# Two mixers and two FFNs on one core: the order of work at the borders, and the place of the state's scaling in the second mixer

## The chip, the core and the metric

The kernel runs on one core of a Trainium2 chip. The metric is the device time of one execution in microseconds (us), as a median over runs. A core has these engines, each with an instruction queue of its own that is worked off strictly in order: PE (matrix products and transposes, results into PSUM), DVE (vector work), ACT (activations, copies), POOL (further vector work, without PSUM) and SP (it issues DMA transfers). An instruction that waits for another engine holds up everything behind it in its own queue. Which engine ends its wait is seen in the profile behind an arrow, for instance "<-DVE u_b L474".

## What is computed

The input x is 4 batches of 1024 rows with 512 columns. Four layers follow each other, each of them added to x:

```python
x = x + mixer_a(layernorm(x))     # 16 heads, state 64, convolution over 4 rows
x = x + ffn(layernorm(x))
x = x + mixer_b(layernorm(x))     # 64 heads, state 128, convolution over 4 rows
x = x + ffn(layernorm(x))         # the same weights
```

A mixer projects the row to a gate z, to channels that go through a short convolution and a silu (h, B and C), and to one step size dt per head. Then a recurrence runs along the rows of a batch, for each head:

```python
state = state * exp(dt * A) + dt * h * B      # outer product
y     = C . state + D * h
```

y is gated with silu(z), normalized (in mixer b the norm comes first and the gate after it), and projected back to 512 columns. The FFN takes the last row of every batch, turns it in four steps of a small network into a "thought", projects that, and adds gate(x) * thought to all rows, then normalizes:

```python
thought = layer_norm(x)[:, -1, :] @ agg_w + agg_b
for _ in range(4):
    thought = thought + gelu(layer_norm(thought) @ d1_w + d1_b) @ d2_w + d2_b
out = x + sigmoid(x @ gate_w + gate_b) * (thought @ bc_w + bc_b)
result = layer_norm(out)
```

## The kernel before

**Stages.** The rows are cut into 32 tiles of 128 (8 to a batch). Mixer A runs from 0 to about 1195 us, the first FFN to about 1388, mixer B to about 2865, the second FFN to the end. Between the stages x goes through DRAM.

**A mixer** works in groups of two tiles ("chunks" c = 0, 1). For each group there is a *norm* (lines 389 to 441: statistics, a root on POOL, line 417 on DVE, the normalized rows on ACT in line 419, transposes on PE) and a *front* (443 to 628: the projections on PE, in pieces; each piece ends with a yield). The front's pieces are gates ("pz", a tanh on ACT, z on DVE in line 541) and convolutions ("pc" on PE, a first tap on ACT in line 470, three taps on DVE in line 474, then a silu). The small products of dt ("pd", line 503) are strung between the large ones. At the end of a front the running sums of dt * A go to DRAM, and *lay_sums* (641) lays them into tables called past and upto, which PE reads.

*chunk* (762) does the recurrence of 128 rows in closed form. Mixer A has wide heads (CG = 2), mixer B narrow ones (CG = 4), and for B the order is this:

1. *decays(0)* (781): PE forms the exponents of the decay masks L of a quarter of the heads in four PSUM banks ("seg"), ACT takes their exponentials (805).
2. The tail of the chunk before (658): the projection back, "pout" and "ssq" on PE.
3. *from_state* (840), in all chunks but the first of a batch: PE multiplies C with the state into two banks "po" (846), DVE scales them by the decay of each row into "yo" (850), two multiplications.
4. On POOL the state and a copy of h ("hdr") are scaled for the next state. Then the first yield: pieces of the next group's front are put in here, until the numbers that they yield have used up the chunk's.
5. *weigh(L0)* (809 to 812): DVE multiplies the masks by the products of B and C, two halves. Behind it come decays(1), the next step of the tail (684 to 690: the residual x and its statistics), a yield with front pieces, and weigh(L1).
6. *open_y* (855): PE turns yo into y's bank (859), and *inner* (817, 828) adds the products of L and h. Masks 2 and 3, the closing of y and the new state ("pst", 897, 908) follow.

So the order on PE, DVE, ACT and POOL inside a mixer is written out by hand: the code's order is the queue's, and no planner changes it. SP's order, and that of the code outside of the manual_schedule blocks, is set by a scheduler. A mixer has seven PSUM banks for all products but y; a product that finds no free bank waits for the reader of the one that it is given.

**At the kernel's start** the tables' constants are made on DVE: eleven reductions of the identity into flags (190), two corrections, two pasts (201, 204) and the flags of upto (*lay_flags*, 208). Of upto there are two, with four sets each; mixer A needs set 0, mixer B all. The call for sets 1 to 3 is in the first FFN (1096), but on the chip all of them run at the start, from 10.4 to 17.0 us, since the scheduler moves them there. Then comes the first norm and the first front, with the whole of mixer A's output weight w_out scaled by its norm weights on ACT in eight instructions ahead of it (317).

**The first FFN** turns twelve tiles (the last of the 32, *filling*) to gates while the thoughts are formed, each of them a transpose (1184), four passes of the gate weight (1196), a bias (1208), a tanh and a store ("sgd"); their last steps are done in mixer B's norm. Then the thought is projected (1225), goes out to DRAM (1229) and comes back on all partitions ("hbc", 1238). The other 20 tiles go through *Tile*, a pipeline of steps over turns: turned, projected, biased, tanh, weighed with hbc (1278), added, measured, centered (1301), left (1304, 1305).

Of the kernel before, what the change touches and what calls it, by code (L numbers as in the profile page):

```python
# [72 lines left out]
def hybrid_kernel(  # L73
# [106 lines left out]

    eye = ident.rearrange("p (r w) -> p r w", w=32)
    flags = const.tile([P, 2 * HB + 3], F32, tag="flags", name="flags")
    for i, at in enumerate(
        [slice(2 + h + 10 * lo, 7 + h + 10 * lo, 4) for lo in (0, 1) for h in range(HB)]
        + [slice(10 * lo, 10 * lo + 2) for lo in (0, 1)]
        + [slice(20, 21)]
    ):
        nc.vector.tensor_reduce(flags[:, i : i + 1], eye[:, :, at], mybir.AxisListType.XY, ALU.add)  # L190
    heads4, first2, row20 = flags[:, :HB], flags[:, 2 * HB : 2 * HB + 1], flags[:, 2 * HB + 2 :]
    nc.vector.scalar_tensor_tensor(
        heads4, flags[:, HB : 2 * HB], 1.0 / LO_SCALE, heads4, ALU.mult, ALU.add
    )
    nc.vector.scalar_tensor_tensor(
        first2, flags[:, 2 * HB + 1 : 2 * HB + 2], 1.0 / LO_SCALE, first2, ALU.mult, ALU.add
    )
    pasts, sums = [], []
    for i in range(2):
        past = const.tile([P, SETS, P], F16, tag=f"past{i}", name=f"past_{i}")  # L200
        nc.vector.tensor_scalar_mul(
            past.rearrange("p t s -> p (t s)"), first2.to_broadcast([P, SETS * P]), -1.0
        )
        nc.vector.tensor_scalar(past[:, :, 64:], past[:, :, 64:], row20, None, ALU.add)
        upto = const.tile([P, SETS, HB, P], F16, tag=f"upto{i}", name=f"upto_{i}")
        pasts.append(past)
        sums.append(upto)
    def lay_flags(sets):
        for upto in sums:
            for t in sets:  # L210
# [6 lines left out]
                    ALU.mult,  # L217
                    ALU.add,
                )

    lay_flags(range(MIX_A.heads // 16))

    def rsqrt(v):

# [24 lines left out]
    def mixer(m, in_w, conv_w, conv_b, dt_bias, A_log, Dv, norm_w, out_w, src, dst, first, stats, last_steps={}):  # L249
# [18 lines left out]
        with stack:  # L268
# [43 lines left out]
            nc.vector.tensor_scalar_min(Ab, Ab, A_LOG_MAX)  # L312
            nc.scalar.activation(Ab, Ab, AF.Exp)
            nc.vector.tensor_scalar_mul(Ab, Ab, -A_SCALE)

            for e in range(KE):
                nc.scalar.activation(w_out[:, e, :], w_out[:, e, :], AF.Identity, scale=nw[:, e : e + 1])

# [441 lines left out]
            def chunk(f, c, following):  # L762
# [72 lines left out]
                        )  # L835
                        started[cg] = True

                tmps = []

                def from_state():  # L840

                    pos = []
                    for half in range(2):
                        rows, hsl = state_at(half)
                        po = mm(f"po_{tag}_{half}")
                        nc.tensor.matmul(po, Cc[rows, cols], state["S"][rows, hsl], start=True, stop=True)  # L846
                        pos.append(po)
                    for half, po in enumerate(pos):
                        tmp = wk.tile([P, 512], F32, tag="yo", name=f"yo_{tag}_{half}", bufs=2)
                        nc.vector.tensor_mul(  # L850
                            heads_of(tmp), heads_of(po), over_head(el[:, half * HALF : (half + 1) * HALF], P, HALF)
                        )
                        tmps.append(tmp)
# [74 lines left out]
                yield 2.0  # L928
                weigh(L0)
                if CG == 4:  # L930
                    L1 = decays(1)
                    next(last, None)
                    yield 2.2
                    weigh(L1)
                    py, on = open_y(0)
                    for half in range(2):
                        inner(0, L0, half, py, on)
                    L2 = decays(2)
                    yield 3.0
                    weigh(L2)  # L940
                    for half in range(2):
                        inner(1, L1, half, py, on)
                    close_y(0, py)
                    to_state()
                    yield 2.2
                    L3 = decays(3)
                    yield 2.8
                    weigh(L3)
                    py, on = open_y(1)
                    for half in range(2):  # L950
                        inner(2, L2, half, py, on)
                    yield 2.2
                    for half in range(2):
                        inner(3, L3, half, py, on)
                    close_y(1, py)
                else:
                    next(last, None)
                    yield 2.5
                    to_state()
                    yield 2.0  # L960
                    for half in range(2):
                        py, on = open_y(half)
                        inner(0, L0, half, py, on)
                        close_y(half, py)
                        yield 3.8
# [14 lines left out]
            with tc.manual_schedule(  # L980
                engines={
                    mybir.EngineType.PE,
                    mybir.EngineType.DVE,
                    mybir.EngineType.Activation,
                    mybir.EngineType.Pool,
                }
            ):
                fs = [Group(*groups[0]), Group(*groups[1])]
                for _ in norm(fs[0], None):
                    pass  # L990
                for _ in front(fs[0], fs[1]):
                    catch_up()
                lay_sums(fs[0], 0)
                for n in range(len(groups)):
                    if n + 2 < len(groups):
                        fs.append(Group(*groups[n + 2]))
                    f, ahead, behind = (fs + [None, None])[n : n + 3]
                    pieces = front(ahead, behind) if ahead is not None else iter(())
                    due = 0.0
                    for c in range(GC):  # L1000
                        following = (f, c + 1) if c + 1 < GC else (None if ahead is None else (ahead, 0))
                        for us in chunk(f, c, following):
                            due += us
                            while due > 0.0:
                                waiting, later_on[:] = later_on[:], []
                                piece = next(pieces, None)
                                for step in waiting:
                                    step()
                                if piece is None:
                                    break  # L1010
                                due -= piece
                            catch_up()
                    for _ in pieces:
                        catch_up()
                state.pop("fold")()
                for _ in state["tail"]:
                    catch_up()
# [3 lines left out]
    def ffn(r, src, dst, stats, filling, bias_on_pe):  # L1021
# [5 lines left out]
        CG = P // 32  # L1027
        KQ = KF // CG
        leaves = r == 0
        stack = ExitStack()  # L1030
        with stack:
            wk = stack.enter_context(tc.tile_pool(name=f"wk_f{r}", bufs=1, reuse_waits="tile"))
# [58 lines left out]
            nc.vector.tensor_copy(ones4, ident[:, 0:NB])  # L1091
            for g in range(1, CG):
                nc.vector.tensor_add(ones4, ones4, ident[:, 32 * g : 32 * g + NB])

            if leaves:
                lay_flags(range(MIX_A.heads // 16, SETS))

            def to_columns(src, n, name):

# [100 lines left out]


            kept = {}
            for i in filling:
                tag = f"{r}_{i}"
                xi = ahead[i] if i in ahead else load_tile(i, f"x_f{tag}")
                ps = project_gate(i, copy_turned(i, turn_tile(i, normed(i, xi, f"xn_f{tag}"))))
# [35 lines left out]


            class Tile:
                def __init__(self, i, resumed):
                    self.i, self.resumed = i, resumed
                    self.tag = f"{r}_{i}"
                    self.x = load_tile(i, f"x_{'g' if resumed else 'f'}{self.tag}")

# [17 lines left out]
                        nc.vector.tensor_add(self.th, self.th, gb)  # L1267

                def tanh(self):
                    if self.resumed:  # L1270
                        self.th = p_c.tile([P, D], F32, tag="c", name=f"th_{self.tag}")
                        nc.scalar.activation(self.th, kept[self.i], AF.Tanh, scale=0.5)
                    else:
                        nc.scalar.activation(self.th, self.th, AF.Tanh, scale=0.5)

                def weigh(self):
                    self.sg = wk.tile([P, D], F32, tag="sg", name=f"sc_{self.tag}", bufs=4)
# [49 lines left out]
            for n, one in enumerate(others):  # L1327
                order.append(one)
                while behind and len(behind) * len(others) > (len(others) - 1 - n) * len(filling):
                    order.append(behind.pop(0))  # L1330
            tiles = {}
            with tc.manual_schedule(
                engines={
# [6 lines left out]
                for t in range(-2, len(order) + 4):  # L1340
                    if t + 2 < len(order):
                        tiles[t + 2] = Tile(*order[t + 2])
                    for step, turn in turns:
                        if t - turn in tiles:
                            step(tiles[t - turn])

            def last_step(i, xi):
# [99 lines left out]
```

## Time and profile before

| | us |
|---|---|
| median of 3 runs | 3091.79 (3088.93 to 3094.5) |
| the profiled execution | 3096.08 |
| its span | 3094.4 |
| busy: PE / DVE / ACT / POOL | 2772.5 / 2094.4 / 1254.0 / 736.2 |
| PE busy from 1440 to 2803 us (mixer B) | 1225.8 of 1363.0 |
| PE busy from 1302 to 1379 us (20 tiles of the first FFN) | 76.5 of 77.0 |
| PE idle ahead of mixer B's first transposes, 1388.24 us | 9.75 |
| PE's first instruction of the kernel starts at | 18.05 |

A line of the timeline has the start, the duration, the engine, the line of the code, the operation, what it writes and reads with the partitions and elements, how often, and in brackets how long the engine stood idle before it and what ended that. Where several instructions of one line follow each other, they are drawn together (x3), with the time of all. A name like po_b or pc_a is the tile's with the mixer's letter. A line of waits has the waiting instruction, the one that it waited for, and the total, the number and the longest of the waits. A duration in the timeline reaches to the end of an instruction's writing, so the next one of the same engine may start a little before it.

### The profile page before, as it was taken

What the parts mean: (1) busy time and instruction counts of PE and PEld (TensorE: products, weight loads), DVE (VectorE), ACT (ScalarE), POOL (GpSimd) and SP (SyncE); (2) the same over time, 40 slices, a digit from 0 to 9 for tenths busy, and PEclk for the clock granted to TensorE, in tenths of its full rate; (3) what the DMA queues carried; (4) which work ended last, traced back from release to release, by engine and by line L of the source; (5) the groups of instructions that cost most, each with busy time, mean ns of one, the idle gap of its engine ahead of it and who ended that gap; (6) DMA issues with size and microseconds to landing.
All of it is one profiled execution on the core that took longest, in us unless ns stands there. A gap on an engine that the chain in (4) does not pass through costs nothing. (4 is left out here: it accounts for less than half of the span.)

```text
span 3094.4 us, 46185 instructions
## 1 busy us (share of the span) xinstructions
PE 2772.5 (90%) x17156; PEld 1775.0 (57%) x17156; DVE 2094.4 (68%) x4417; ACT 1254.0 (41%) x2874; POOL 736.2 (24%) x839
## 2 busy tenths in 40 slices
PE   6999999999999998989999889999888998898986
PEld 5666666666666664347665656666555665554332
DVE  4677666667766663286677777776787777876358
ACT  3333433333334333255344444444444443444245
POOL 1222122112222221170221112112223212212157
PEclk9999999999999998999999999999999999998999
DMA  3000000000000014430000000000000000001423
GB/s 115 9 20 20 16 16 16 16 16 16 23 17 16 13 67 167 162 124 10 20 13 20 19 17 11 20 20 20 20 25 16 26 20 19 17 10 72 167 87 108
DMA packets 92960, 124.27 MB, mean 40 GB/s; under 512 B 38728, under 2 KB 42328, under 8 KB 92736
## 3 DMA queue, kind: packets, MB, share of 16 engines
q1 hardware_dynamic: 80960, 98.23, 9.9%
q10 hardware_dynamic: 9792, 16.82, 1.4%
q0 software_dynamic: 1984, 6.26, 0.6%
q8 instruction: 137, 2.24, 0.3%
q14 instruction: 87, 0.71, 0.1%
HBM read 84.54 MB, written 36.72 MB: 39 GB/s over the span
## 5 line engine op out<-in xcount | busy, mean ns | idle before, releaser
L347 PE MATMUL pc_b<-xnT_b,w_in_b 128*128 128x259 f32 x1280 | 356.3, 404 | 22.3 <-DVE u_b L474 22.3
L347 PE MATMUL pc_a<-xnT_a,w_in_a 128*128 128x259 f32 x1152 | 312.0, 395 | 0.0
L812 DVE TENSOR_TENSOR L_b<-L_b,Gm_b 128x1024 f32<-128x1024 f32 x256 | 308.6, 1248 | 2.9 <-ACT L_b L805 2.9
L347 PE MATMUL pz_a<-xnT_a,w_in_a 128*128 128x256 f32 x1024 | 300.1, 407 | 0.7 <-ACT xnT_a L436 0.7
L347 PE MATMUL pz_b<-xnT_b,w_in_b 128*128 128x256 f32 x1024 | 294.0, 395 | 3.5 <-ACT xnT_b L436 3.5
L805 ACT ACTIVATE L_b<-seg_b 128x512 f32<-128x512 f32 x512 | 262.9, 599 | 65.5 <-PE seg_b L798 63.8
L347 PEld LDWEIGHTS pc_b<-xnT_b,w_in_b 128*128 128x128 f32 x1280 | 228.4, 199 | 103.0 <-issue 41.6
L474 DVE SCALAR_TENSOR_TENSOR u_b<-pc_b,cw_b,u_b 128x256 f32<-128x256 f32 x480 | 231.4, 482 | 82.3 <-ACT u_b L470 70.9
L669 PE MATMUL pout_a<-w_out_a,h_a 128*128 128x512 f32 x512 | 253.3, 642 | 34.9 <-DVE u_a L474 34.9
L1196 PE MATMUL g_ps<-gw,xnT_f 128*128 128x512 f32 x512 | 249.7, 625 | 6.5 <-DMA gw<-in_L_ffn_gate_w 4.2
L828 PE MATMUL py_b<-L_b,hdt_b 128*32 128x128 f32 x4096 | 161.4, 289 | 91.8 <-DVE L_b L812 89.5
L474 DVE SCALAR_TENSOR_TENSOR u_a<-pc_a,cw_a,u_a 128x256 f32<-128x256 f32 x432 | 208.2, 482 | 50.2 <-ACT u_a L470 39.1
L669 PE MATMUL pout_b<-w_out_b,h_b 128*128 128x512 f32 x512 | 236.1, 604 | 0.0
L347 PEld LDWEIGHTS pc_a<-xnT_a,w_in_a 128*128 128x128 f32 x1152 | 195.0, 191 | 69.1 <-issue 23.7
L881 POOL TENSOR_TENSOR h_b<-h_b,z_b 128x256 f32<-128x256 f32 x128 | 91.1, 733 | 468.4 <-ACT sq_b L880 468.4
L347 PEld LDWEIGHTS pz_a<-xnT_a,w_in_a 128*128 128x128 f32 x1024 | 168.5, 193 | 39.0 <-issue 8.6
L347 PEld LDWEIGHTS pz_b<-xnT_b,w_in_b 128*128 128x128 f32 x1024 | 167.0, 191 | 40.1 <-issue 18.2
L470 ACT ACTIVATE u_a<-pc_a,cb_a,cw_a 128x256 f32<-128x256 f32 x144 | 81.1, 564 | 263.8 <-PE pc_a L347 199.1
L828 PEld LDWEIGHTS py_b<-L_b,hdt_b 128*32 128x32 f32 x4096 | 106.2, 113 | 141.2 <-DVE L_b L812 74.0
L669 PEld LDWEIGHTS pout_a<-w_out_a,h_a 128*128 128x128 f32 x512 | 99.3, 204 | 146.3 <-issue 143.6
L1196 PEld LDWEIGHTS g_ps<-gw,xnT_f 128*128 128x128 f32 x512 | 94.5, 198 | 121.2 <-issue 115.7
L669 PEld LDWEIGHTS pout_b<-w_out_b,h_b 128*128 128x128 f32 x512 | 92.4, 190 | 99.3 <-issue 99.1
(320 smaller groups left out, 4945.8 us busy)
## 6 DMA issues: line engine op xcount, KB each, us to landing
d<-in_L_ffn_d_w SPq DMA_DIRECT2D x4, 2048.0 KB
x_f<-xa SPq DMA_DIRECT2D x32, 256.0 KB
xb<-x_b ACTq DMA_DIRECT2D x32, 256.0 KB
x_f<-xb SPq DMA_DIRECT2D x32, 256.0 KB
x_a<-in_L_attn_a_x SPq DMA_DIRECT2D x30, 256.0 KB
xa<-x_a ACTq DMA_DIRECT2D x30, 256.0 KB
out<-x_f SPq DMA_DIRECT2D x22, 256.0 KB
xf<-x_f SPq DMA_DIRECT2D x20, 256.0 KB
```

Source lines behind the costliest of these rows:

```text
L347: nc.tensor.matmul(*args, **kw)
L470: nc.scalar.activation(u, ps[:, 0:GT], AF.Identity, bias=cb[:, j : j + 1], scale=cw[:, j, 0:1])
L474: nc.vector.scalar_tensor_tensor(u, ps[:, k : k + GT], cw[:, j, k : k + 1], u, ALU.mult, ALU.add)
L669: nc.tensor.matmul(pout, f.hs[e // 2][:, e % 2, cols], w_out[:, e, :], **on)
L805: nc.scalar.activation(L[:, r], sg[r0 + r], AF.Exp)
L812: nc.vector.tensor_mul(Lr, Lr, Gm.unsqueeze(1).to_broadcast([P, 2 * HB, P]))
L828: nc.tensor.matmul(py[cg * CT : (cg + 1) * CT, e % 4, :], hdt[:, h // HC, u : u + HC, :], Ls[half][:, r, hq, :], start=not started[cg], st ...
L881: nc.gpsimd.tensor_mul(yh, yh, zs[half * 2 + r][:, :, cols])
L1196: nc.tensor.matmul(ps, xnT[:, k, :], gw[:, k, :], start=(k == 0), stop=(k == KD - 1 and not bias_on_pe))
```

## The change

Four edits:

1. At the start, the flags and pasts become a function *lay_constants*, called behind the first norm; set 0 of upto follows it, and sets 1 to 3 are laid behind the first front and its lay_sums.
2. The scaling of w_out becomes a generator *weigh_rows*: one of the eight instructions after each piece of the first front of a mixer, from the seventh piece on.
3. In mixer B the scaling of the state's part (line 850) is a function of its own, *scale_state*, and is called after weigh(L0). Mixer A calls it where it was.
4. In the first FFN the last two of the twelve gates are no longer made ahead of the thought's projection but as gate-only tiles at the end of the pipeline.

```diff
-    for i, at in enumerate(
...
-    lay_flags(range(MIX_A.heads // 16))
...
+    def lay_constants():
+        eye = ident.rearrange("p (r w) -> p r w", w=32)
...
-            for e in range(KE):
-                nc.scalar.activation(w_out[:, e, :], w_out[:, e, :], AF.Identity, scale=nw[:, e : e + 1])
+            def weigh_rows():
+
+                for e in range(KE):
+                    nc.scalar.activation(w_out[:, e, :], w_out[:, e, :], AF.Identity, scale=nw[:, e : e + 1])
+                    yield
...
-                tmps = []
+                pos, tmps = [], []
 
                 def from_state():
 
-                    pos = []
                     for half in range(2):
                         rows, hsl = state_at(half)
                         po = mm(f"po_{tag}_{half}")
                         nc.tensor.matmul(po, Cc[rows, cols], state["S"][rows, hsl], start=True, stop=True)
                         pos.append(po)
+                    if CG < 4:
+                        scale_state()
+
+                def scale_state():
                     for half, po in enumerate(pos):
                         tmp = wk.tile([P, 512], F32, tag="yo", name=f"yo_{tag}_{half}", bufs=2)
...
                 weigh(L0)
                 if CG == 4:
+                    scale_state()
                     L1 = decays(1)
...
-                for _ in front(fs[0], fs[1]):
+                if first:
+                    lay_constants()
+                    lay_flags(range(TS))
+                weighing = weigh_rows()
+                for at, _ in enumerate(front(fs[0], fs[1])):
                     catch_up()
+                    if at >= 6:
+                        next(weighing, None)
+                for _ in weighing:
+                    pass
                 lay_sums(fs[0], 0)
+                if first:
+                    lay_flags(range(TS, SETS))
...
+        last = 2 if leaves else 0
...
-            if leaves:
-                lay_flags(range(MIX_A.heads // 16, SETS))
-
...
-            for i in filling:
+            for i in filling[: len(filling) - last]:
...
                 def tanh(self):
-                    if self.resumed:
+                    if self.gate_only:
+                        self.keep()
+                    elif self.resumed:
...
+                def keep(self):
+
+                    sg = wk.tile([P, D], F32, tag="sg", name=f"sg_{self.tag}", bufs=4)
+                    nc.scalar.activation(sg, self.th, AF.Tanh, scale=0.5)
+                    kept[self.i] = dr.tile([P, D], F32, tag=f"sg{self.i}", name=f"sgd_{self.tag}")
+                    nc.sync.dma_start(kept[self.i], sg)
...
+            order += [(i, False, True) for i in filling[len(filling) - last :]]
+            gate_steps = (Tile.turn, Tile.project, Tile.add_bias, Tile.tanh, Tile.copy, Tile.normalize)
...
-                        if t - turn in tiles:
+                        if t - turn in tiles and (not tiles[t - turn].gate_only or step in gate_steps):
                             step(tiles[t - turn])
```

The two programs have the same instructions on PE, DVE, ACT, POOL and SP; only their order differs.

More of the change, by code (lines that the diff above doesn't have):

```diff
@@ L175, in hybrid_kernel @@
     SETS = max(MIX_A.heads, MIX_B.heads) // 16
-    eye = ident.rearrange("p (r w) -> p r w", w=32)
     flags = const.tile([P, 2 * HB + 3], F32, tag="flags", name="flags")
-    for i, at in enumerate(
[L186 to L190, printed above, removed]
-    heads4, first2, row20 = flags[:, :HB], flags[:, 2 * HB : 2 * HB + 1], flags[:, 2 * HB + 2 :]
@@ L192, in hybrid_kernel @@
[L192 to L202, printed above, removed]
-        )
[L204 to L207, printed above, removed]
+    heads4, first2, row20 = flags[:, :HB], flags[:, 2 * HB : 2 * HB + 1], flags[:, 2 * HB + 2 :]
@@ new lines, in hybrid_kernel @@
+    pasts = [const.tile([P, SETS, P], F16, tag=f"past{i}", name=f"past_{i}") for i in range(2)]
+    sums = [const.tile([P, SETS, HB, P], F16, tag=f"upto{i}", name=f"upto_{i}") for i in range(2)]
+    def lay_constants():
+        eye = ident.rearrange("p (r w) -> p r w", w=32)
+        for i, at in enumerate(
+            [slice(2 + h + 10 * lo, 7 + h + 10 * lo, 4) for lo in (0, 1) for h in range(HB)]
+            + [slice(10 * lo, 10 * lo + 2) for lo in (0, 1)]
+            + [slice(20, 21)]
+        ):
+            nc.vector.tensor_reduce(flags[:, i : i + 1], eye[:, :, at], mybir.AxisListType.XY, ALU.add)
+        nc.vector.scalar_tensor_tensor(
+            heads4, flags[:, HB : 2 * HB], 1.0 / LO_SCALE, heads4, ALU.mult, ALU.add
+        )
+        nc.vector.scalar_tensor_tensor(
+            first2, flags[:, 2 * HB + 1 : 2 * HB + 2], 1.0 / LO_SCALE, first2, ALU.mult, ALU.add
+        )
+        for past in pasts:
+            nc.vector.tensor_scalar_mul(
+                past.rearrange("p t s -> p (t s)"), first2.to_broadcast([P, SETS * P]), -1.0
+            )
+            nc.vector.tensor_scalar(past[:, :, 64:], past[:, :, 64:], row20, None, ALU.add)
@@ L1244, in ffn, with __init__ @@
             class Tile:
-                def __init__(self, i, resumed):
-                    self.i, self.resumed = i, resumed
+                def __init__(self, i, resumed, gate_only=False):
+                    self.i, self.resumed, self.gate_only = i, resumed, gate_only
                     self.tag = f"{r}_{i}"
```

## The prediction, made before the changed kernel ran

> **What bounds the kernel now.** I read the page first, then the waits of PE and DVE inside the second mixer, then the timelines of the places that the diff touches. The page puts PE at 90% busy, DVE at 68%, ACT at 41%: PE sets the time, so a saved or added microsecond counts only where PE stands still. That happens at the borders (the start, the seam between the first FFN and mixer B) and, in small doses, in every chunk of mixer B. These are PE's longest waits in mixer B between 1440 and 2803 us (total, times, longest):
>
> ```profile
> PE py_b L828 <- DVE L_b L812: 81.0, 87, 4.8
> ...
> PE pc_b L347 <- DVE u_b L474: 22.3, 15, 1.5
> ```
>
> So in mixer B PE's first lack is the weighed mask L of line 812, which DVE makes. Anything put ahead of a weighing on DVE is to be suspected, anything taken from ahead of it is welcome. The change does both, at different places.
>
> **Mixer B: the state's scaling (two multiplications of line 850) goes behind the first weighing.** Before, DVE does them as soon as PE has made po. The question is whether DVE had something else to do there. DVE in an odd chunk (start, duration, instruction, idle before it and what ended it):
>
> ```profile
> 1922.30 0.42 DVE L971 TENSOR_TENSOR sq_b<-sq_b 128x256 f32<-128x256 f32 x1
> 1925.31 0.69 DVE L850 TENSOR_TENSOR yo_b<-po_b,ea_b 128x512 f32<-128x512 f32 x1 [2.59 <-PE po_b L846]
> ...
> 1929.45 1.52 DVE L474 SCALAR_TENSOR_TENSOR u_b<-pc_b,cw_b,u_b 128x256 f32<-128x256 f32 x3 [2.59 <-ACT u_b L470]
> ...
> 1932.34 2.35 DVE L812 TENSOR_TENSOR L_b<-L_b,Gm_b 128x1024 f32<-128x1024 f32 x2
> 1934.61 0.14 DVE L684 TENSOR_SCALAR rs_b<-rs_b 128x1 f32<-128x1 f32 x1
> ...
> 1938.50 2.35 DVE L812 TENSOR_TENSOR L_b<-L_b,Gm_b 128x1024 f32<-128x1024 f32 x2
> ```
>
> The two scalings sit in a hole: 2.59 us of idleness ahead, 2.59 us behind (1.7 to 2.9 in the other chunks), because the next DVE work is the front's convolution, which waits for ACT and PE. The weighing stays behind that convolution in both programs. So the hole gets larger and the weighing at 1932.34 starts no sooner. In the new place, between 1934.61 and the second weighing, DVE is dense. Two scalings of 0.69 us hold DVE 0.61 each (a 0.69 us z at 1885.17 is followed by the next instruction at 1885.78): 1.22 us later for line 684, for the residual and its statistics, and for the second weighing. PE in the same chunk:
>
> ```profile
> 1931.12 0.68 PE L347 MATMUL pc_b<-xnT_b,w_in_b 128*128 128x259 f32 x2 [1.49 <-DVE u_b L474]
> ...
> 1933.39 0.60 PE L859 MATMUL py_b<-ident,yo_b 128*128 128x128 f32 x4
> ...
> 1939.77 0.64 PE L828 MATMUL py_b<-L_b,hdt_b 128*32 128x128 f32 x16 [1.10 <-DVE L_b L812]
> 1940.90 0.65 PE L828 MATMUL py_b<-L_b,hdt_b 128*32 128x128 f32 x16 [0.49 <-DVE L_b L812]
> ```
>
> Line 859 turns the scaled state into y, so it now waits for the scaling: from 1933.39 to about 1935.3 (1934.61 + 0.69). That by itself puts only PE's next 6 us back. What lasts is the next wait: PE is at 1939.77 already 1.10 us early for the second weighing, and this comes 1.22 us later. From 1942 to 1968 PE has no further wait, so nothing takes it back: **+1.22 us** an odd chunk.
>
> An even chunk (DVE, then PE):
>
> ```profile
> 1885.78 2.35 DVE L812 TENSOR_TENSOR L_b<-L_b,Gm_b 128x1024 f32<-128x1024 f32 x2
> ...
> 1895.17 1.52 DVE L474 SCALAR_TENSOR_TENSOR u_b<-pc_b,cw_b,u_b 128x256 f32<-128x256 f32 x3 [1.08 <-ACT u_b L470]
> ```
> ```profile
> 1888.04 0.61 PE L859 MATMUL py_b<-ident,yo_b 128*128 128x128 f32 x4
> ```
>
> The weighing ends at 1888.05, the first scaling at 1888.74, so line 859 starts some 0.8 us late and with it the pc products behind it on PE. DVE's own 1.22 are partly swallowed by its idle 1.08 at 1895.17, but not below the 0.8 by which that convolution's pc is late. Later PE waits there (0.94 + 0.49 for the third weighing) hang on DVE, so the 0.8 stays: **+0.8 us**.
>
> There are 28 chunks with an earlier state. Two, in the last group, have no front between po and the weighing: there L's weighing really goes into the wait for po (4.81 and 7.41 us long), and of PE's waits for L812 (1.75 and 1.42 in one, 0.51, 0.49 and 2.50 in the other) I take 2 us off each: -4. The other 26 are 15 odd and 11 even: 15 x 1.22 + 11 x 0.8 = 27.1. Together **+23**. Bounds: -4 if PE gains the 26 delays back elsewhere; +61 if each pays 2.5, its 1.22 and another 1.3 by the banks: po's two PSUM banks are held 7 to 9 us longer, and the next pc then takes a bank that is freed by line 679 (1932.27) and not by the convolution (end 1930.97). I keep near the middle, since that 1.3 lies within the wait of line 859. A gain from a DVE that no longer stands before po is excluded in the 26 by the idle behind the scaling, 1.7 us or more everywhere.
>
> **The start.** One row each of DVE, ACT, ACT and DVE:
>
> ```profile
> 17.00 0.22 DVE L417 SCALAR_TENSOR_TENSOR mv_a<-mv_a 128x1 f32<-128x1 f32 x2
> ```
> ```profile
> 17.18 1.52 ACT L419 ACTIVATE xn_a<-x_first,mv_a 128x512 f32<-128x512 f32 x2 [11.56 <-DVE mv_a L417]
> ...
> 35.84 5.01 ACT L317 ACTIVATE w_out_a<-w_out_a,nw_a 128x512 f32<-128x512 f32 x8 [15.19 <-DMA w_out_a<-in_L_attn_a_out_proj_w]
> ```
> ```profile
> 47.91 0.69 DVE L396 BATCH_NORM_STATS2 st_a<-x_a 128x6 f32<-128x512 f32 x1
> ```
>
> The norm's last small step, line 417, stands behind all the flags (9.47 to 17.0). Put ahead of them it needs only POOL's root (done at 10.4): 6.6 us earlier for xn, the transposes and the first gates. ACT then meets no scaling of w_out (wait until 35.84, then 5.01) before its first tanh: 40.75 becomes about 24.5, and DVE, idle for 10.02 us before 41.35, goes on to line 396, which needs the next two tiles of x. These were issued on SP behind w_out; the DMA moved 237 GB/s in 34-36, 91 in 36-38 and 8 in 38-40 us, so they land at about 36.5. From 47.91 on DVE is dense up to 66.8 and the rest follows it: 47.91 - 36.5 = 11.4 earlier. The eight scalings (0.63 each) now stand between ACT's convolution starts; I charge 0.9 for the ones that come ahead of a u. The twelve flag instructions of sets 1 to 3 (4.5 us) go behind the first front, where DVE is idle from 76.56 to 81.65; without that cover they cost up to 4.5. **-10.5** (-12 to -6).
>
> A sentence of the Trainium skill reads differently here: "TensorE: Matmul & The Clock Gate", Part 1, has PE at full clock after some 3.4 us of busy time, whereas two pz and two pd take 1.28 us all the way from 20.7 to 30.9 and 0.65 after 75, with a granted clock of 1.00 shown. By the page, as an estimate, these 10.2 us would end some 3.4 us sooner; since x lands at 36.5, the sum is the same by either.
>
> **The end of the first FFN.** PE, and the window in which thoughts turn into the broadcast row (its last columns are PE's clock, the DMA share and GB/s):
>
> ```profile
> 1371.23 7.25 PE L1196 MATMUL g_ps<-gw,xnT_f 128*128 128x512 f32 x16
> 1388.24 1.94 PE L434 MATMUL tpx_b<-ident,xn_b 128*128 128x128 f32 x8 [9.75 <-DVE sign_b L331]
> ```
> ```profile
> 1286.00:1302.00 16.00, 14.56 (x49) 6.27 (x49) 3.63 (x6) 4.27 (x8) 0.00 (x0) 1.00 0.89 338
> ```
>
> PE does the same work, only two gates (7.1 us at 1288.35, and their transposes) go from ahead of the broadcast to behind the last whole tile. That tile's long tail on DVE, ACT and POOL (mixer B's first PE work waits for its end, 9.75 us) then runs beside the gates; what remains behind PE's end is a bias (0.70), a tanh, a centering (0.69) and leaves of 1.4: about 3.9 us. That is -5.8. On the other side the row hb goes out and back by DMA (issue 1299.75 to the reload at 1301.5 and its landing), now some 7 us earlier, when w_in_b and w_out_b are still on their way (0.89 busy, 338 GB/s, until about 1299); the first weighing waits for it, PE for its bank, 0.8 us. **-5** (-7 to -2).
>
> Against this edit speaks a line of the Trainium skill, "Trainium Kernel Development and Optimization", Key Constraints: all queues share the same 16 DMA engines. Taken as a strict line-up, hb would come no earlier than now and, as an estimate, half the gain would go; the trace has nothing that shows it.
>
> **The scaling of w_out in mixer B**, 1394.60 to 1399.61 on ACT, was beside PE's first gates and is now spread over the front's pieces: +0.5 (0 to 1.5; without cover 5.0).
>
> **The sum.** -10.5 - 5 + 0.5 + 23 = +8. The profiled execution took 3096.1 us (span 3094.4 and 1.7 around it); it is 4.3 above the median of the three runs. On the median, 3091.8 + 8 = **3100**.
>
> **Rivals.**
> - *The delays are swallowed (faster).* In the 26 chunks the scaling's 1.22 us fall into DVE's later gaps (1.08 before a convolution; 2.01 and 1.53 before the z of odd chunks), and PE's waits behind them shrink as much. For it: DVE is idle some 11 us a chunk. Against it: the L waits come before those gaps. Scaling at 0 gives 3091.8 - 15 = 3077; full gain in the last group 3073. It decides from the point where the move costs under 9 us in all, a third of my 27.
> - *The banks bite (slower still).* po held longer stops seg or pc for another 1 us: 26 more, 3126. For it: PE already waits 22.3 us for banks read by line 474.
> - *The borders bring half*: x late, hb held up by the weights: -8 in place of -15, 3107.
>
> **Chances.** My forecast 0.50, swallowed 0.26, banks 0.17, borders 0.07. Three tenths of my own case's spread (+-10) lie within 0.2% of the time, 6 us, about what can be told from no change; so faster 0.26, same 0.15, slower 0.59. The range goes from swallowed (3072) to most of the banks (3122).
>
> **What would show it.** Right: line 419 at about 10.6, line 396 at about 36.5; 3.9 and not 9.75 us before the first tpx_b; the wait "py_b L828 <- L812" up from 81 towards 100, a new wait of py_b L859 for the scaling; the idle before u_b in odd chunks 6.7 and not 2.59 us (both holes and the scalings in one). Wrong: L812 starting sooner than 7 us behind po, or PE's waits in mixer B not growing.

## The result and the profile after

The changed kernel takes 3110.95 us (median of 4 runs, 3108.26 to 3113.98) against 3091.72: ratio 1.0062, 95% interval 1.0046 to 1.0077, so 14 to 24 us slower. The forecast was 3100, slower by 8, with a range from 3072 to 3122.

The profiled execution (span 3106.6 us) can be cut at two instructions of PE: the first transpose of the first FFN and the first one of mixer B.

| stage | before | after | difference | forecast |
|---|---|---|---|---|
| to the first FFN (the start) | 1198.91 | 1186.56 | -12.3 | -10.5 |
| first FFN (the gates) | 189.33 | 185.11 | -4.2 | -5 |
| mixer B (the scaling, w_out) | 1476.9 | 1507.2 | +30.3 | +23.5 |
| second FFN to the end | 229.3 | 227.7 | -1.6 | 0 |

The borders gained about what they should (the start's 12.3 is more than its mean over the runs, see below), and the moved scaling took it back twice over. Where in mixer B it did so looks different from what was foretold. PE's waits there, from 1420 to 2860 us:

```profile
PE py_b L828 <- DVE L_b L812: 71.8, 68, 4.8
PE seg_b L788 <- DVE u_b L474: 27.3, 15, 1.9
...
PE pc_b L347 <- DVE rs_b L679: 9.8, 15, 0.7
```

Over the same window of the kernel before, the wait for the masks was 89.5 us: it has *fallen*, while the forecast had it rise. A new one has come, of seg for a bank that the convolution frees. In all, PE stands still in mixer B for 162.9 us and not 157.2, which is 6 us of the 30. The other 24 are in PE's busy time (1319.7 to 1344.3 us) with the same instructions. An odd chunk shows how. DVE first:

```profile
1927.53 1.52 DVE L474 SCALAR_TENSOR_TENSOR u_b<-pc_b,cw_b,u_b 128x256 f32<-128x256 f32 x3 [8.42 <-ACT u_b L470]
...
1930.42 2.35 DVE L812 TENSOR_TENSOR L_b<-L_b,Gm_b 128x1024 f32<-128x1024 f32 x2
1932.69 1.28 DVE L853 TENSOR_TENSOR yo_b<-po_b,ea_b 128x512 f32<-128x512 f32 x2
...
1937.77 2.35 DVE L812 TENSOR_TENSOR L_b<-L_b,Gm_b 128x1024 f32<-128x1024 f32 x2
```

As foretold, the hole ahead of the convolution is now in one piece (8.42 us here; 6.72, as foretold, in an odd chunk in which PE makes po at full clock), the first weighing starts no sooner behind it, and the second one is later: 7.35 us behind the first, 6.16 before. PE beside it:

```profile
1929.11 0.41 PE L788 MATMUL seg_b<-later,ident 64*64 64x256 bf16 x4 [1.73 <-DVE u_b L474]
1929.44 0.40 PE L798 MATMUL seg_b<-upto,past 21*128 21x512 f16 x4
1930.56 0.83 PE L347 MATMUL pc_b<-xnT_b,w_in_b 128*128 128x259 f32 x2 [0.72 <-DVE rs_b L679]
...
1931.39 1.07 PE L347 MATMUL pc_b<-xnT_b,w_in_b 128*128 128x259 f32 x2
...
1940.18 0.64 PE L828 MATMUL py_b<-L_b,hdt_b 128*32 128x128 f32 x16 [0.19 <-DVE L_b L812]
```

Two pc products take 1.07 us here, 0.60 before. The windows of this stretch (the columns are the stretch, its length, five engines' busy time, PE's granted clock, DMA share, GB/s) say why:

```profile
1930.00:1932.00 2.00, 1.45 (x5) 1.16 (x6) 1.97 (x5) 1.93 (x4) 1.42 (x1) 0.75 0.00 0
1932.00:1934.00 2.00, 2.00 (x8) 1.41 (x7) 2.00 (x4) 0.00 (x0) 0.04 (x1) 0.50 0.00 0
1934.00:1936.00 2.00, 2.00 (x39) 1.50 (x37) 1.81 (x6) 1.27 (x3) 0.00 (x0) 0.90 0.13 51
```

PE's clock is halved from 1931.0 to 1934.4 (such a stretch is called a *spell* below), behind waits of 0.45, 1.73 and 0.72 us. So when PE gets to the second mask it hardly waits (0.19 us, where it was 1.10 + 0.49): it has been slow in the meantime. Over windows of 4 us, what each lacks of the full clock, doubled, adds up to 104 us at half clock in mixer B before and 150 after.

That leaves two readings, and the profile alone can't decide between them. **Theory DVE queue** (the forecast's): the scalings put 1.2 us more into DVE's dense stretch, so every second mask is 1.2 us later, and the slow clock only fills time in which PE would have waited. **Theory banks and clock** (the rival): po's two banks, held until the scaling, stop PE; its clock falls, and that is the loss.

### The profile page after: what moved, and what is told of

It is laid out like the page before. It is cut to its first block, busy times and chain, and to the rows that moved or that the text cites. A ratio compares the mean times of both kernels' runs of the same rounds, so it can differ in the third digit from the quotient of the medians.

```text
span 3106.6 us, 46192 instructions
## 1 busy us (share of the span) xinstructions
PE 2793.6 (90%) x17156; PEld 1791.2 (58%) x17156; DVE 2090.1 (67%) x4417; ACT 1253.4 (40%) x2874; POOL 734.5 (24%) x839
## 5 line engine op out<-in xcount | busy, mean ns | idle before, releaser
L347 PE MATMUL pc_b<-xnT_b,w_in_b 128*128 128x259 f32 x1280 | 378.8, 422 | 15.6 <-DVE rs_b L679 9.8
L347 PEld LDWEIGHTS pc_b<-xnT_b,w_in_b 128*128 128x128 f32 x1280 | 238.4, 208 | 100.9 <-issue 38.6
```

The lines of the kernel that those rows point to most:

```text
L347: nc.tensor.matmul(*args, **kw)
```

## The experiments

Mixer B's length, PE's idle time in it and the time at half clock are from the profiled run of each kernel; the last two columns are times from po to po in the second batch (odd chunks 1, 3 and 5, even chunks 2 and 4).

| kernel | median us | ratio to before, 95% interval | mixer B | PE idle | half clock | odd chunks | even chunks |
|---|---|---|---|---|---|---|---|
| before | 3091.72 | | 1476.9 | 157.2 | 104 | 41.87 41.88 41.87 | 46.78 46.67 |
| after | 3110.95 | 1.0062 (1.0046-1.0077) | 1507.2 | 162.9 | 150 | 43.07 44.77 43.50 | 47.95 47.85 |
| e1 scaling only | 3122.20 | 1.0091 (1.0076-1.0107) | 1508.1 | 163.4 | 156 | 43.07 43.67 44.77 | 47.97 47.87 |
| e2 borders only | 3078.78 | 0.9954 (0.9939-0.9969) | 1476.3 | 159.0 | 99 | 41.87 41.87 41.87 | 46.76 46.68 |
| e3 occupancy | 3147.54 | 1.0175 (1.0158-1.0192) | 1528.9 | 200.5 | 122 | 43.20 44.14 44.15 | 48.10 48.00 |
| e4 banks | 3114.97 | 1.0066 (1.0051-1.0082) | 1498.1 | 164.3 | 129 | 42.15 42.95 43.97 | 47.22 46.94 |
| e5 wait | 3099.03 | 1.0022 (1.0010-1.0034) | 1482.0 | 165.7 | 98 | 41.99 42.01 42.00 | 46.90 46.81 |
| e6 last group | 3077.72 | 0.9949 (0.9933-0.9965) | 1473.6 | 160.1 | 92 | 41.88 41.88 41.88 | 46.77 46.67 |
| e7 fill | 3108.68 | 1.0054 (1.0035-1.0072) | 1506.9 | 164.0 | 81 | 43.08 43.07 43.08 | 47.98 47.88 |
| e8 one moved | 3110.52 | 1.0063 (1.0042-1.0084) | 1497.7 | 159.0 | 136 | 42.47 44.17 42.49 | 47.37 47.28 |
| e9 weighing behind | 3073.38 | 0.9932 (0.9916-0.9948) | 1474.2 | 147.1 | 140 | 42.39 42.12 43.67 | 45.43 45.33 |
| e10 weighing ahead | 3036.88 | 0.9815 (0.9799-0.9830) | 1435.7 | 133.0 | 85 | 41.29 40.36 40.36 | 45.43 45.34 |

The ratios are to the runs of the kernel before on the same chip (its median was 3091.72, 3095.33, 3091.34 and 3097.14 us in the four groups of runs).

**e1: the scaling alone**, the kernel before with the third edit only.

> The kernel before with the move of the state's scaling alone. In the changed kernel mixer B got 30 us longer (from the first tpx_b to the second FFN's first transpose). All theories that see this loss in the moved scaling expect about 3092 + 30 = 3122 us. If part of the loss came from the other three edits (another phase of the clock, w_out's scaling in pieces), it is less: 3105 to 3115.

Mixer B is as long as in the changed kernel (1508.1 and 1507.2). The whole loss is the scaling's.

**e2: the borders alone**, the changed kernel with the scaling back.

```diff
-                    if CG < 4:
-                        scale_state()
+                    scale_state()
...
-                    scale_state()
                     L1 = decays(1)
```

> The changed kernel with the scaling of the state back at its old place, so the three border edits alone. In the trace the first FFN starts 12.4 us earlier and mixer B another 4.2, so theory one (the borders gain, the scaling loses) expects 3092 - 16.6 + 0 to 3 for w_out's pieces in mixer B: about 3076. If the borders' gain is lost again in mixer B whatever the scaling does: 3085 to 3092.

3078.78, 16.5 us under the median of the kernel before on its chip (14 by the ratio), near the 16.6 that was expected. Mixer B has its old length.

**e3: DVE's queue alone.** Everything stays at its place, but two statistics over the scaled state are put behind the first weighing.

```diff
                 if CG == 4:
+                    for half, tmp in enumerate(tmps):
+                        spare = wk.tile([P, 8], F32, tag="spare", name=f"spare_{tag}_{half}", bufs=1)
+                        nc.vector.bn_stats(spare[:, 0:6], tmp)
                     L1 = decays(1)
```

> The kernel before, with two idle-purpose statistics over the scaled state (128x512, about 0.6 us each on DVE) behind the first weighing in mixer B; their results are used by nothing. PSUM banks, PE's waits for yo and the scaling's place are as before: only DVE's queue is longer there. Theory DVE queue (1.2 us later for the second weighing, and PE waits for that in every chunk): 28 x 1.2 = 34, so about 3125. Theory banks (the loss comes from po's two PSUM banks being held, which stops PE and lets its clock fall): little, 3092 to 3100.

The two take 1.42 us together and hold DVE 1.33; the even chunks of the table and its first odd chunk, in which PE's clock stays up, are longer by exactly that, and the wait for the masks is what grows:

```profile
PE py_b L828 <- DVE L_b L812: 116.4, 98, 5.2
```

It cost more than expected, 52 us and not 34. The difference is in chunks with spells (the two odd ones of the table pay 2.27, single ones elsewhere up to 3.9). In such a chunk PE waits in one piece for the second mask and is slow just behind it:

```profile
1952.56 2.21 PE L828 MATMUL py_b<-L_b,hdt_b 128*32 128x128 f32 x32 [2.43 <-DVE L_b L812]
```

These 32 products take 1.08 us at full clock; from 1952.5 to 1955 the granted clock was 0.50.

**e4: the held banks alone.**

```diff
                 if CG == 4:
+                    for half, po in enumerate(pos):
+                        spare = wk.tile([P, 8], F32, tag="spare", name=f"spare_{tag}_{half}", bufs=1)
+                        nc.vector.tensor_copy(spare[:, 0:1], po[:, 0:1])
                     L1 = decays(1)
```

> The kernel before with the scaling at its old place, but behind the first weighing DVE also copies one column of each po (results unused, about 0.1 us each), so that only the two PSUM banks stay held as long as in the changed kernel. Theory DVE queue: 26 x 0.2 at most, 3092 to 3097. Theory banks: in the 15 odd chunks PE waits about 1.7 us for a bank that line 474 frees, and its clock halves now and then: 3092 + 15 x 1.2 to 15 x 2, about 3110 to 3122.

The kernel is some 20 us slower, with the same new waits as in the changed kernel:

```profile
PE seg_b L788 <- DVE u_b L474: 27.3, 15, 1.9
PE pc_b L347 <- DVE rs_b L679: 10.3, 15, 0.7
```

In the table the even chunks lose 0.3 to 0.4, the odd ones anything between 0.3 and 2.1, as the clock falls or not. Not all of that is the banks' doing: the two copies hold DVE for 0.26 us, about what the chunks without spells lose, or 7 us over 28 chunks. So the banks by themselves cost some 14 us. Each of the two mechanisms is enough for a loss, and e3 and e4 don't add up to e1 (52 + 21 against 31).

**e5: the wait of line 859 alone.**

```diff
                 if CG == 4:
+                    for tmp in tmps:
+                        nc.vector.tensor_copy(tmp[:, 0:1], tmp[:, 0:1])
                     L1 = decays(1)
```

> The kernel before with the scaling at its old place, and behind the first weighing DVE copies one column of each scaled part onto itself (about 0.1 us each), so that only PE's line 859 has to wait as long as in the changed kernel. po's banks are free early. Theory DVE queue: 26 x 0.2 at most, up to 3098 us. If the wait of line 859 is a cost of its own (0.8 us in even, 1.9 in odd chunks, not hidden): 3092 + 26 x 0.8 to 26 x 1.4, 3113 or more.

Line 859 waits 21.4 us in all for these copies, but a chunk gets only 0.12 us longer, what the copies take on DVE. The wait by itself lies beside the later one for the second mask, as the forecast had it. So does a spell: each of the three odd chunks has one of 3.4 us here, and is no longer for it.

**e7: keep PE busy while it waits for the bank.** In the changed kernel:

```diff
                     for r in range(4):
+                        if CG == 4 and t == 1 and r == 2 and c == 1 and i < NT - GC:
+                            fill = p_y.tile([P, 4, P], F32, tag="y", name=f"fill_{tag}")
+                            for n in range(14):
+                                nc.tensor.transpose(fill[:, n % 4, :], ident, ident)
```

> The changed kernel with 14 PE transposes of the identity (results unused, about 1.6 us) put into the stretch of the odd chunks of mixer B in which PE waits for a bank that line 474 frees. They do no work that is needed. If PE's clock falls because PE stands still there, the half-speed spells of mixer B go from 28 back to about 18. Theory DVE queue (the 1.2 us on DVE set the chunk, the spells lie beside them): 3108 to 3111, little change. Theory clock (the spells cost by themselves, PE busy rose by 25 us): 10 to 20 us faster, 3091 to 3101, although PE does more.

This one decides between the two. The wait for the bank is covered by the 1.75 us of transposes, the clock stays up (the same stretch as above, in this kernel)

```profile
1931.00:1933.00 2.00, 1.23 (x11) 0.64 (x11) 1.90 (x8) 1.12 (x3) 0.40 (x1) 1.00 0.00 0
1933.00:1935.00 2.00, 2.00 (x12) 1.36 (x10) 2.00 (x3) 0.95 (x2) 1.06 (x1) 1.00 0.00 0
```

and mixer B spends 81 us at half clock and not 150, yet it is as long as in the changed kernel (1506.9 and 1507.2). PE gets to the second mask early again and waits:

```profile
1941.06 0.64 PE L832 MATMUL py_b<-L_b,hdt_b 128*32 128x128 f32 x16 [0.62 <-DVE L_b L816]
1942.20 0.65 PE L832 MATMUL py_b<-L_b,hdt_b 128*32 128x128 f32 x16 [0.49 <-DVE L_b L816]
```

Without slow spells every chunk of the second batch, odd or even, is 1.19 to 1.21 us longer than in the kernel before: the time that two scalings hold DVE. So DVE's queue sets the loss. Bank waits and slow clock lie beside it, in some chunks wholly and in others in part: the changed kernel's odd chunks of the table pay 1.2 to 2.9 us. Over the whole mixer these extras nearly cancel, since the kernel before had spells as well; four of its odd chunks were 1.7 us longer for them. That the lengths of mixer B in e7 and in the changed kernel agree to 0.3 us is partly luck: e7 is 3.8 us shorter up to the third batch and 3.5 longer behind it, where six of its chunks pay 1.7 to 3.3 us.

**e8: half the dose**, only the second scaling moved (`scale_state(0)` at the old place, `scale_state(1)` behind the weighing).

> The kernel before with only the second of the two scalings behind the first weighing in mixer B. Theory DVE queue: half the queue, 26 x 0.6 less some 3 in the last group, about 13 us over the kernel before, 3105. Theory banks: one bank held in place of two, so the loss depends on whether that is the one that stops PE: either near 0 or near the whole 20.

Even chunks are longer by 0.6, half of 1.2, and so are the odd ones with a single spell (42.47, 42.49). The second bank alone also brings the wait for line 474 (26.6 us) and further spells (the odd chunk of 44.17 has two), so that mixer B is 20.8 us longer; 13 was expected. Over e5, e8, the changed kernel and e3 an even chunk pays 0.12, 0.6, 1.2 and 1.33 us, each time what was put on DVE.

**e6: the move only where it has no front behind it**, in the two chunks of the last group.

```diff
+                late = CG == 4 and i >= NT - GC
...
-                    if CG < 4:
+                    if not late:
                         scale_state()
...
-                    scale_state()
+                    if late and not begin:
+                        scale_state()
```

> The changed kernel with the moved scaling only in the two chunks of mixer B's last group, where no front pieces stand between po and the weighing; elsewhere the old place. Theory: the three border edits alone gave 16.5 us under the kernel before; these two chunks give another 4 (2 each): about 20 under the kernel before, near 3074. If the move never pays: no better than 16 under it.

Mixer B is 2.7 us shorter than in e2 by the traces (1473.6 and 1476.3), not 4, in one execution of each; the run times of e6 and e2 can't be told apart.

**e9 and e10: weigh the masks in the hole.** If DVE's dense stretch is what counts, it isn't the scaling that should move but the weighing, out of the stretch. Both are the borders of e2 and, in mixer B, weigh(L0) ahead of the first yield: in e9 behind the scaling, in e10 ahead of it, in the wait for po.

```diff
                 def from_state():
...
+                    if CG == 4:
+                        weigh(L0)
                     scale_state()
...
                 if not begin:
                     from_state()
+                elif CG == 4:
+                    weigh(L0)
...
                 yield 2.0
-                weigh(L0)
+                if CG < 4:
+                    weigh(L0)
```

> The border edits alone, and in mixer B the first weighing of the masks put right behind the scaling, ahead of the front pieces: into DVE's hole (1.9 to 2.9 us after the scaling), out of the dense stretch that ends in the second weighing. Theory DVE queue: 2.27 us less ahead of the second weighing, so PE's waits for it (1.10 + 0.49 in odd chunks, 0.43 in even ones) go: 15 x 1.5 + 11 x 0.4 = 27, some of it lost where the convolution behind the hole is put off by 0.4; 3078 - 18 to - 27, 3051 to 3060 us. Theory that the place on DVE matters little and banks and clock decide: 3075 to 3080.

> The border edits alone, and in mixer B the first weighing put ahead of the scaling, both ahead of the front pieces, so that it runs while DVE waits for po (2.59 us in odd, 4.81 in even chunks). Theory DVE queue: as with the weighing behind the scaling, but nothing is put off behind it, since 2.27 us fit into the wait: 3051 to 3058 us, and 2 us each in the last group. Theory banks and clock: 3075 to 3080.

e10 is 1.85% faster than the kernel before (3036.88 us), better than expected; e9 gains some 7 us on e2 by the ratios (whose intervals overlap) and 2 in mixer B, less than expected. DVE in an odd chunk of e10:

```profile
1895.77 0.42 DVE L978 TENSOR_TENSOR sq_b<-sq_b 128x256 f32<-128x256 f32 x1
1896.11 2.35 DVE L812 TENSOR_TENSOR L_b<-L_b,Gm_b 128x1024 f32<-128x1024 f32 x2
1898.78 0.69 DVE L854 TENSOR_TENSOR yo_b<-po_b,ea_b 128x512 f32<-128x512 f32 x1 [0.31 <-PE po_b L845]
...
1902.91 1.52 DVE L474 SCALAR_TENSOR_TENSOR u_b<-pc_b,cw_b,u_b 128x256 f32<-128x256 f32 x3 [2.59 <-ACT u_b L470]
```

The weighing fills the 2.59 us of waiting for po to 0.31, and the convolution behind starts as long after po as before. In e9 the weighing comes behind the scaling; its two halves reach over 3.65 us there (2.35 elsewhere), the convolution starts late, PE's wait for a bank freed by line 474 grows to 35.7 us, and the clock falls (140 us at half). What stands beside the slow weighing is POOL's scaling of the state:

```profile
1902.53 1.94 POOL L929 TENSOR_TENSOR S_b<-S_b,ea_b 128x1024 f32<-128x1024 f32 x1 [10.53 <-PE po_b L845]
...
1903.03 3.65 DVE L812 TENSOR_TENSOR L_b<-L_b,Gm_b 128x1024 f32<-128x1024 f32 x2
```

Of the 256 halves of weighings in e9, 31 take twice their time, 24 of them beside this scaling; in the kernel before there are 7, one of them beside it. In neither does a half that meets this scaling take its usual time. No run moves POOL's work away, so that it is the cause is not shown.

## Why the forecast was right, and where its steps were not

The direction and the main mechanism were right. The size was not: +8 was foretold and +19 measured, and the three large terms below all erred to the same side.

- **The scaling in mixer B, +23 (measured +30.3).** The mechanism holds: in 26 chunks the scaling leaves a hole and enters a dense stretch. The step that failed is the even chunk's "+0.8", with DVE's 1.22 us "partly swallowed by its idle 1.08". Measured: 1.17 and 1.18. Line 859 starts 0.74 us later, as foretold (0.52 of it from a pc that waits for a bank that z frees), but the idle 1.08 was no slack. The convolution's first tap on ACT stands in ACT's queue behind line 753, which waits for DVE's own Gm (line 751), and Gm comes right behind the second weighing. So DVE waits there for the outcome of its own late work, and the 1.08 us move with it. Before, then after:

```profile
1893.80 0.28 DVE L751 TENSOR_TENSOR Gm_b<-misc_b,le 128x128 f32<-128x128 f32 x1
...
1894.18 0.33 ACT L753 ACTIVATE ea_b<-misc_b 128x192 f32<-128x192 f32 x1 [1.48 <-DVE Gm_b L751]
...
1894.55 0.58 ACT L470 ACTIVATE u_b<-pc_b,cb_b,cw_b 128x256 f32<-128x256 f32 x1
```
```profile
1890.20 0.28 DVE L751 TENSOR_TENSOR Gm_b<-misc_b,le 128x128 f32<-128x128 f32 x1
...
1890.58 0.33 ACT L753 ACTIVATE ea_b<-misc_b 128x192 f32<-128x192 f32 x1 [1.88 <-DVE Gm_b L751]
...
1890.95 0.58 ACT L470 ACTIVATE u_b<-pc_b,cb_b,cw_b 128x256 f32<-128x256 f32 x1
...
1891.56 1.52 DVE L474 SCALAR_TENSOR_TENSOR u_b<-pc_b,cw_b,u_b 128x256 f32<-128x256 f32 x3 [1.08 <-ACT u_b L470]
```

  That is some 4 us over 11 even chunks.
- **The odd chunk, +1.22.** That is right to 0.02 us where the clock stays up (e7: 1.20). With spells, odd chunks of the changed kernel pay up to 2.9, a cost that the sum did not have.
- **The last group, -4.** Measured -2.7 (e6 against e2).
- **What would show it.** Here the forecast was wrong: PE's waits for the masks were to rise to 100 us, and fell; "PE's waits in mixer B not growing" was named as a sign against it, and they grew by 6 us only. The sign was badly chosen: PE's wait had been turned into slow work. e7, which takes the slow work away, brings the wait back (82.4 us for the masks and 8.4 for yo, 1420 to 2860) at the same length. The new wait of line 859 for the scaling, also named as a sign, comes to 0.8 us in the changed kernel; e7's 8.4 us are that wait.
- **"The banks bite"** was priced at 26 us on top of the rest. Alone they cost some 14 us (e4 without what its copies hold DVE). On top of the queue little is left of that in sum (e7), as the forecast's sentence on the other wait had it, though single chunks pay up to 1.7 us more; the rival's sum was wrong.
- **The start, -10.5.** Line 419 starts at 9.99 (foretold 10.6), line 396 at 36.65 (foretold 36.5), and DVE then waits for the tile of x, as foretold:

```profile
36.65 0.69 DVE L396 BATCH_NORM_STATS2 st_a<-x_a 128x6 f32<-128x512 f32 x1 [2.63 <-DMA x_a<-in_L_attn_a_x]
```

  By the second chunk's first product of B and C (81.51 before) the lead is 9.8 us, in e2 8.5. At the end of mixer A it is less on average: the first FFN starts at 1189.5 us in the mean of the six profiled runs with the edit (1185.7 to 1194.0) and at 1196.7 in six without it (1194.2 to 1199.7), 7.2 earlier. Some 3 us get lost on the way, in a mixer whose code is the same; where, I did not test.
- **The end of the first FFN, -5 (measured -4.2).** The tail is as foretold: PE stands still 3.80 us (foretold 3.9) ahead of mixer B. The step that failed is hb's way through DRAM, priced at 0.8:

```profile
1290.08 0.69 DVE L1299 SCALAR_TENSOR_TENSOR sc<-g_ps,hbc 128x512 f32<-128x512 f32 x1 [5.75 <-DMA hbc<-hbd]
```
```profile
1290.82 3.70 PE L1208 MATMUL g_ps<-gw,xnT_f 128*128 128x512 f32 x8 [2.99 <-DVE sc L1299]
...
1371.67 1.94 PE L434 MATMUL tpx_b<-ident,xn_b 128*128 128x128 f32 x8 [3.80 <-DVE sign_b L331]
```

  PE pays 2.99 us. From hb's store to its reload SP needs 6.31 us (1280.24 to 1286.55), 1.40 before, while the weights of mixer B load. This is the side on which the Trainium skill's line on the shared DMA engines stood ("Trainium Kernel Development and Optimization", Key Constraints). The strict line-up that the prediction made of it (the page itself has the transfers interleave) was too dark: hb was late by some 5 us, but a gain remained. Store, reload and most of the weights are also issued on one queue, SP's; whether the engines or the queue held hb up, no run separates.
- **w_out in pieces, +0.5.** Mixer B of e2 is as long as before in all (1476.3 and 1476.9). Its stretch up to the first po, in which the pieces lie, is 1.0 us longer (94.91 and 93.93); that can be the pieces or the tail of the FFN beside them.
- **The clock at the start.** The prediction read a granted clock of 1.00 beside slow products; that reading is wrong (see the end).

The sum with the measured terms, -7.2 - 4.2 + 30.3 = +19, is the runs' difference.

## What to carry to other kernels

Before an instruction is moved in an in-order queue, look at both ends: it frees nothing if a hole surrounds it, and it costs its whole time where the queue is dense and the engine that sets the time waits for the end of that stretch. The useful question is the reverse one: what in the dense stretch could run in the hole? Here that was the weighing: put into the hole, ahead of the scaling, it turned +19 us into about -60 (e10, with the borders). One place further on, behind the scaling, most of that gain was gone (e9), so look also at what other engines do in the hole. Idle time in front of an instruction is slack only if what it waits for doesn't hang on the same queue's earlier work. And a wait that shrinks is no proof of a gain: look whether the waiting engine's own work has become slower.

## What the hardware showed

PE's clock falls to half for 3.4 us at a time (1920.8 to 1924.2 and 1931.0 to 1934.4 in the changed kernel), after no single wait of more than 1.73 us. In the 3.4 us ahead of these two spells PE stood still for 1.60 and 2.23 us. The amount alone does not decide: in this trace stretches of that length with 1.51 us of standing still were followed by a spell, and one with 1.86 was not. The Trainium skill ("TensorE: Matmul & The Clock Gate", Part 1) has a free-running window of about 3.4 us for this; the length of the spells agrees, and e7 shows that useless transposes in the gap keep the clock up.

On the same page PE is at full clock after one busy window. At the start of the changed kernel two pz and two pd take 1.28 us for 10.2 us without a break, though the windows show 1.00 as granted. That 1.00 is only the lack of a record: the trace's record of the clock begins at 26.4 us (32.0 in the kernel before), and at that moment the spacing of the pc products falls from 0.43 to 0.22 us. So PE ran at half speed from its first transpose at 10.85 us on, for some 15.5 us with one wait of 0.68 in them. That is longer than the page's window, and why stays unexplained here.
